# Full attention of a four-layer kernel: a new timetable of its tasks by beats, scores' two uses 24 beats apart, biases added by TensorE

## The chip, the cores and the metric

The kernel runs on one core of a Trainium2 chip. The metric is device time in microseconds (us) of one execution; a kernel is run several times and the median is compared.

## The reference

The input x has 16 batches of 512 tokens with 128 features. Four residual layers follow one another, each of the form x = x + layernorm(layer(layernorm(x))): windowed attention with 16 heads, a feed-forward layer with eight experts, full attention with 16 heads of 8 features, and a feed-forward layer with a sine. Only the third is changed:

```python
qkv = x @ Wqkv + bqkv                      # x: layernorm of the residual
q, k, v = split into 16 heads of 8         # rope on q and k
attn = softmax(q @ k.T * 8 ** -0.5)        # 512 x 512 for each head and batch, no mask
out = (attn @ v) joined to 128 features
return out @ Wout + bout
```

## The kernel before

The four layers run one after another. The third, `full_attention` (L873), works through the 16 batches with an order written out by hand: a loop over **beats** (L1161), 32 to a batch. Engines aren't locked to beats. A beat only says in which order instructions go into each engine's own queue, and every queue then runs in that order, as soon as what it waits for is there. SP (SyncE) has such a queue too, for nearly all transfers of this layer. I call the 32 beats in which batch b is attended the frame of b, and count beats 0 to 31 in it; z is the half of the heads (z=0 or 1).

In each beat three things run on the main road:

- `attend` (L1094): two matmuls (L1104) make scores transposed, with keys on partitions, and ScalarE (ACT) takes their exponential (L1110). Beats 0 to 15 use z=0, beats 16 to 31 use z=1.
- `score` (L1061) of a later batch: two matmuls (L1070) make the same scores with queries on partitions, and VectorE (DVE) takes each row's greatest (L1073). So scores are used twice: here for the maximum, and 32 beats later in `attend`, which gets the maximum as two extra rows of the contraction. I call these 32 beats the lead.
- `products` (L1113), every second beat: eight matmuls (L1118) multiply exponentials with values; a column of ones in the values gives the sums. It runs three beats behind.

Beside these, tasks are started at certain beats. They are generators; `yield n` puts what follows n beats later, and `run_due` (L202) goes through the tasks that are due at the end of each beat.

- `arrive(b+3)` (L966), from beat 10: GpSimd (POOL) gathers the experts' rows (`hb`, four indirect transfers, L972), makes `y` (four operations, L978), adds them (L983), normalizes (`normed_in`, L175: statistics by DVE, power and scaling by POOL) and adds to x (L986).
- `project(b+2)` (L988), from beat 0: normalizes x by POOL, transposes it (`tp_f`, L995, beat 6), multiplies with the weights (`pqk`, L1002, beat 8; bias by ACT in `qk`, L1008), makes values (`pv`, L1013, beat 10; bias by DVE into `vs`, L1017), and turns q and k by rope: three POOL operations for each of two halves (L1029 to L1032, beats 10 and 13). Each half is then cut into a high part (DVE, L964) and a rest (POOL, `cut`, L1035) and written to memory (`away`, L1038). From there 16 transfers of 128 KB load it in the layout that the scores need: four `qs` and four `ks` for z=0 (beat 20) and as many for z=1 (beat 23), all at L1056. Five pairs of buffers `qs`, `ks` go round. Zeroing them (L936, L937) is done while the experts run.
- `greatest(b+1, z)` (L1075), after the last score of a half (beats 15 and 31): a transpose (`pm`, L1081), a cut into `hi_m` and `lo_m` by DVE, and four small transfers that write these rows into `qs` (L1090).
- `put_away` (L1123), beats 2, 10, 18, 26: ACT copies products (`ou`, L1127), SP writes them (`heap`, L1128).
- `output(b-1)` (L1130), from beat 2: reads back sums and products (`sc`, `oc`, L1135, L1137, beat 4), DVE takes reciprocals (`rc`, L1140, beat 8), which go out and come back spread (`far`, `rb`, L1143, L1144), POOL multiplies (`oT`, L1147, beat 14), TensorE (PE) multiplies with the output weights (`pf`, L1151, beat 16), DVE adds the bias (`o`, tile `fo`, L1153), then `normed_in` and the residual sum (L1156).

One more thing orders the work. In the built program SP's transfers of this layer share eight completion semaphores in turn: with few exceptions a transfer isn't issued before the eighth transfer ahead of it has landed, and everything behind it in SP's queue waits too. `score` and `pm` take turns in two tiles of PSUM, so `score` of one beat waits for the `nm` reduction two tiles earlier.

Of the kernel before, what the change touches and what calls it, by code (L numbers as in the profile page):

```python
# [31 lines left out]
P = 128  # L32
# [142 lines left out]
def normed_in(net, x4, name, out, scale=None, mul=1.0, add=LN_EPS):  # L175
# [11 lines left out]
    nc.vector.tensor_scalar(v, mv[:, :, 1], mul, add, op0=ALU.mult, op1=ALU.add)  # L187
    r = net.small.tile([P, k], F32, name=f"r_{name}", tag="cr")
# [684 lines left out]
def full_attention(net):  # L873
# [20 lines left out]
    with ExitStack() as ctx:  # L894
# [15 lines left out]
        for half in range(2):  # L910
# [8 lines left out]
        vbias = wp.tile([P, 1, H1 * D1], F32, name="vbias")  # L919
        nc.sync.dma_start(  # L920
            out=vbias[:, 0, :], in_=a["L1_attn_bqkv"].rearrange("(o n) -> o n", o=1)[:, 2 * C :].to_broadcast([P, C])
        )
        wo = wp.tile([P, C], F32, name="wo1")
        nc.sync.dma_start(out=wo, in_=a["L1_attn_Wout"])
        bout = wp.tile([P, 1, C], F32, name="bout")
        nc.sync.dma_start(
            out=bout[:, 0, :], in_=a["L1_attn_bout"].rearrange("(o c) -> o c", o=1).to_broadcast([P, C])
        )
        ones_row = net.ones[: H1, :]

        qs = [wp.tile([P, HQ, T], F32R, name=f"qs{i}") for i in range(5)]
        ks = [wp.tile([P, HQ, T], F32R, name=f"ks{i}") for i in range(5)]
        for i in range(5):
            for r in range(2):

                nc.gpsimd.memset(qs[i][64 * r + 32 : 64 * r + 64, :, :].bitcast(F32), 0.0)  # L936
                nc.gpsimd.memset(ks[i][64 * r + 32 : 64 * r + 64, :, :].bitcast(F32), 0.0)  # L937
                for k in range(2):
                    nc.sync.dma_start(
                        out=ks[i][64 * r + KR + k : 64 * r + KR + k + 1, :, :].bitcast(F32), in_=ones_row  # L940
                    )
# [24 lines left out]
        def arrive(b):  # L966
# [3 lines left out]
            for j in range(NTB):  # L970
# [4 lines left out]
                )  # L975
            y = tok.tile([P, NTB, C], F32, name=f"y_{b}", tag="z")
# [5 lines left out]
            yield 11  # L982
            nc.gpsimd.tensor_tensor(y, y, hb, ALU.add)  # L983
            yield 4
            yield from normed_in(net, y, f"eo{b}", y)
            nc.gpsimd.tensor_tensor(xb, xb, y, ALU.add)  # L986

        def project(b):  # L988

            z = tok.tile([P, NTB, C], F32, name=f"z_f{b}", tag="z")  # L990
            yield from normed_in(net, net.x[b], f"f{b}", z)
            yield 3
# [19 lines left out]
            for i in range(NTB):  # L1012
                nc.tensor.matmul(  # L1013
                    pv[:, i, :], lhsT=zT[:, i * P : (i + 1) * P], rhs=raw[:, 2].rearrange("c h d -> c (h d)"),
                    start=True, stop=True,
                )
            nc.vector.tensor_tensor(  # L1017
                vs[b % 3][:, :, : VW * H1].rearrange("p i (h d) -> p i h d", d=VW)[:, :, :, :D1],
                pv.rearrange("p i (h d) -> p i h d", d=D1),
                vbias.to_broadcast([P, NTB, C]).rearrange("p i (h d) -> p i h d", d=D1),  # L1020
                ALU.add,
            )
            away = dp.tile([2, 2, 2, 2, 2, HD * HQ, T], F32, name=f"away_{b}", tag="away")
            cuts = []
            for half in range(3):

                if half < 2:
                    t1 = rp.tile([P, T], F32, name=f"t1_{b}_{half}", tag=f"t1{half}")
                    nc.gpsimd.tensor_tensor(t1, side[half], rope[:, 0, :], ALU.mult)  # L1029
                    t2 = rp.tile([P, T], F32, name=f"t2_{b}_{half}", tag="t2")  # L1030
                    nc.gpsimd.tensor_tensor(t2, side[1 - half], rope[:, 1, :], ALU.mult)  # L1031
                    nc.gpsimd.tensor_tensor(t1, t1, t2, ALU.add if half else ALU.subtract)  # L1032
                if half:
                    cut, t = cuts[-1]
                    nc.gpsimd.tensor_tensor(cut[:, 1, :], t, cut[:, 0, :], ALU.subtract)  # L1035
                    yield 1
                    for i in range(2):
                        nc.sync.dma_start(  # L1038
                            out=away.rearrange("k r z p h n t -> (k r z) n p h t")[:, :, i, half - 1, :],
                            in_=cut[:, i, :],  # L1040
                        )
                if half < 2:
                    yield 3
                    cut = rp.tile([P, 2, T], F32, name=f"cut_{b}_{half}", tag=f"cut{half}")
                    halves(cut[:, 0, :], t1)
                    cuts.append((cut, t1))
            yield 2
            for z in range(2):
                for kind, to in enumerate((qs, ks)):
                    for r in range(2):  # L1050

                        of = away[kind, r, z].rearrange("p h (d s) t -> p (h d) (s t)", s=HQ)
                        for i in range(2):
# [3 lines left out]
                                out=to[(2 * b + z) % 5][at : at + 2 * D1, :, :].bitcast(F32), in_=part  # L1057
# [3 lines left out]
        def score(b, k):  # L1061

            z, s, i = k // (HQ * NTB), k // NTB % HQ, k % NTB
            q, kk = qs[(2 * b + z) % 5], ks[(2 * b + z) % 5]
# [10 lines left out]
        def greatest(b, z):  # L1075
# [11 lines left out]
            for r in range(2):  # L1087
                for j, part in enumerate((hi, lo)):
                    at, of = 64 * r + KR + j, r * HQ * NTB
                    nc.sync.dma_start(  # L1090
                        out=qs[(2 * b + z) % 5][at : at + 1, :, :].bitcast(F32), in_=part[of : of + HQ * NTB, :]
                    )

        def attend(b, k):  # L1094
# [4 lines left out]
            q, kk = qs[(2 * b + s // HQ) % 5], ks[(2 * b + s // HQ) % 5]  # L1099
# [30 lines left out]
        def output(b):  # L1130
# [14 lines left out]
            yield 6  # L1145
# [4 lines left out]
            for j in range(NTB):  # L1150
                nc.tensor.matmul(pf[:, j, :], lhsT=oT[:, j * P : (j + 1) * P], rhs=wo, start=True, stop=True)  # L1151
            o = tok.tile([P, NTB, C], F32, name=f"fo_{b}", tag="fo")
            nc.vector.tensor_tensor(o, pf, bout.to_broadcast([P, NTB, C]), ALU.add)  # L1153
            yield 1
            yield from normed_in(net, o, f"fo{b}", o)
# [3 lines left out]
        BEATS = 2 * NG * NTB  # L1159
        with tc.manual_schedule():  # L1160
            for beat in range(-3 * BEATS, (B + 1) * BEATS):  # L1161
                b, k = divmod(beat, BEATS)

# [7 lines left out]
                if 0 <= b + 1 < B:  # L1171
                    score(b + 1, k)
                    if k % (BEATS // 2) == BEATS // 2 - 1:
                        tasks.append([beat, greatest(b + 1, 2 * k // BEATS)])
                if 0 <= pb < B and pk % 2 == 0:
                    products(pb, pk // 2)
                if k == BEATS - 22 and b + 3 < B:
                    tasks.append([beat, arrive(b + 3)])
# [161 lines left out]
```

## Time and profile before

| what | us |
|---|---|
| median of 3 runs | 2868.42 (2852.17 to 2899.47) |
| profiled execution: own time, span | 2889.88, 2888.1 |
| windowed attention, about 0 to 1110 | 1110 |
| experts, about 1110 to 1500 | 390 |
| full attention until its first attended beat, 1500 to 1634 | 134 |
| full attention, attended beats, 1634 to 2674 | 1040 |
| end of the last output, sine layer, 2674 to 2888 | 214 |

In the 1040 us of the attended beats the engines were busy: PE 889.90, DVE 693.29, ACT 593.83, POOL 401.94 us; the mean granted clock of PE was 0.81 of full speed. Busy shares are means over a batch, and PE's busy time includes stretches at half clock, so they do not show what a batch waits for. For that I read the waits of each engine, the chain of waits (what released what, followed back from the end), and the timeline of one batch. Beat 16 of batch 0 starts at 1673.5 us, beat 16 of batch 14 at 2583.8 us: 910.3 us for 14 batches. From batch 1 to batch 13 the distance is 65.2 us on average (62.0 to 68.4).

### The profile page before, as it was taken

How to read it: one execution, taken by the hardware profiler on the slowest of the kernel's cores; microseconds unless marked ns; L12 is line 12 of the kernel's file. 1: busy time of each engine (PE TensorE's matmuls, PEld its weight loads, DVE VectorE, ACT ScalarE, POOL GpSimd, SP SyncE). 2: the span in 40 equal slices, each digit the busy share in tenths (PEclk: the TensorE clock that was granted, in tenths of full speed). 3: DMA queues.
4: the chain of work that ended last, by engine and by line, in shares of the span. 5: the costliest groups of instructions: out<-in, count | busy, mean ns of one | idle time of the engine just before them, and what ended most of it. 6: DMA issues, size and time to landing. Idle time of an engine off the chain costs nothing. (4 is left out here: it accounts for less than half of the span.)

```text
span 2888.1 us, 54880 instructions
## 1 busy us (share of the span) xinstructions
PE 2252.4 (78%) x21335; PEld 1271.2 (44%) x21335; DVE 1865.8 (65%) x3711; ACT 1391.5 (48%) x3176; POOL 1410.3 (49%) x1399
## 2 busy tenths in 40 slices
PE   5888888989888882377771698888888888888676
PEld 2555555555555551366670233333333333332354
DVE  3676777777777754865411767667677767671576
ACT  1545554555455540232330156555555556566685
POOL 2555566565655546433324335444444444410598
PEclk7999999999999995576895568888888888896788
DMA  6555555555555531011112223223323323220001
GB/s 176 165 167 146 162 166 161 155 169 150 163 151 168 163 102 46 18 39 41 47 42 48 55 68 82 76 75 84 80 76 81 84 78 80 74 69 29 22 22 34
DMA packets 164288, 275.45 MB, mean 95 GB/s; under 512 B 20418, under 2 KB 64956, under 8 KB 158908
## 3 DMA queue, kind: packets, MB, share of 16 engines
q1 hardware_dynamic: 157696, 259.41, 31.5%
q0 software_dynamic: 4096, 8.40, 1.0%
q10 hardware_dynamic: 2236, 4.12, 0.5%
q8 instruction: 169, 2.77, 0.4%
q14 instruction: 91, 0.75, 0.1%
HBM read 133.55 MB, written 114.03 MB: 86 GB/s over the span
## 5 line engine op out<-in xcount | busy, mean ns | idle before, releaser
L1073 DVE TENSOR_REDUCE nm<-s 128x2 f32<-128x1024 f32 x512 | 613.4, 1221 | 207.5 <-PE s L1070 159.4
L1110 ACT ACTIVATE ex<-sT 128x512 f32<-128x512 f32 x1024 | 538.3, 601 | 400.9 <-PE sT L1104 388.1
L380 POOL TENSOR_TENSOR t<-t,t 128x512 f32<-128x512 f32 x256 | 319.6, 1269 | 381.4 <-DVE t L377 324.3
L431 ACT ACTIVATE pr<-s,nmax 128x96 f32<-128x96 f32 x1024 | 251.6, 356 | 324.5 <-DVE nmax L425 321.2
L1104 PE MATMUL sT<-qs,ks 50*128 50x512 f32 x1024 | 371.8, 548 | 37.1 <-ACT ex L1110 36.5
L1070 PE MATMUL s<-ks,qs 48*128 48x512 f32 x1024 | 315.3, 502 | 91.2 <-DMA ks<-away 63.8
L1118 PE MATMUL po<-ex,vs 128*32 128x512 f32 x2048 | 336.4, 736 | 0.0
L1104 PEld LDWEIGHTS sT<-qs,ks 50*128 50x128 f32 x1024 | 150.7, 212 | 386.0 <-ACT ex L1110 250.0
L371 PE MATMUL pq<-xnT,wqk 128*128 128x512 f32 x512 | 271.8, 656 | 23.3 <-DVE t L377 21.6
L375 DVE TENSOR_TENSOR t<-pq,rope 128x1024 f32<-128x1024 f32 x128 | 156.5, 1223 | 165.3 <-DMA far<-t 101.2
L443 POOL TENSOR_TENSOR pr<-pr,rc 128x768 f32<-128x768 f32 x128 | 188.0, 1468 | 55.1 <-DVE rc L442 49.8
L1070 PEld LDWEIGHTS s<-ks,qs 48*128 48x128 f32 x1024 | 137.6, 221 | 132.7 <-issue 74.0
L456 ACT COPY prT<-pt 96x512 f32<-96x512 f32 x256 | 138.8, 603 | 115.2 <-PE pt L454 115.2
L392 PE MATMUL pv<-wv,xnT 128*128 128x512 f32 x256 | 152.6, 681 | 29.0 <-ACT v_odd L396 29.0
L377 DVE TENSOR_TENSOR t<-pq,rope 128x1024 f32<-128x1024 f32 x128 | 155.5, 1215 | 0.0
L425 DVE TENSOR_REDUCE nmax<-s 128x8 f32<-128x768 f32 x128 | 118.2, 924 | 53.6 <-PE s L420 53.5
L454 PE MATMUL pt<-ident,pr 64*96 64x64 f32 x2048 | 85.7, 225 | 78.3 <-POOL pr L443 78.2
L485 PE MATMUL pf<-wo,oT 128*128 128x128 f32 x1024 | 131.1, 282 | 15.1 <-ACT v_odd L396 15.1
L371 PEld LDWEIGHTS pq<-xnT,wqk 128*128 128x128 f32 x512 | 92.9, 202 | 113.6 <-issue 97.0
L485 PEld LDWEIGHTS pf<-wo,oT 128*128 128x128 f32 x1024 | 124.2, 195 | 33.3 <-ACT v_odd L396 17.3
L725 PE MATMUL ph<-xT,w 128*128 128x128 f32 x512 | 97.6, 351 | 50.5 <-ACT hT L752 32.9
L471 PEld LDWEIGHTS po<-prT,v_even 96*64 96x64 f32 x2048 | 103.5, 137 | 75.7 <-issue 38.1
(258 smaller groups left out, 4158.2 us busy)
## 6 DMA issues: line engine op xcount, KB each, us to landing
far<-t SPq DMA_DIRECT2D x256, 256.0 KB
kT<-far SPq DMA_DIRECT2D x64, 512.0 KB
qT<-far SPq DMA_DIRECT2D x64, 512.0 KB
away<-cut SPq DMA_DIRECT2D x64, 256.0 KB
qs<-away SPq DMA_DIRECT2D x128, 128.0 KB
ks<-away SPq DMA_DIRECT2D x128, 128.0 KB
heap<-ou SPq DMA_DIRECT2D x64, 256.0 KB
v_even<-v_odd SPq DMA_DIRECT2D x32, 384.0 KB
```

What stands on the lines that cost most here:

```text
L371: nc.tensor.matmul(ps[:, s], lhsT=wqk[:, kind, 2 * half + g, s, :], rhs=xnT[b][:, :T], start=True, stop=True)
L375: nc.vector.tensor_tensor(t1, ps, rope[:, 0:1, :].to_broadcast([P, 2, T]), ALU.mult)
L377: nc.vector.tensor_tensor(t2, ps, rope[:, 1:2, :].to_broadcast([P, 2, T]), ALU.mult)
L380: nc.gpsimd.tensor_tensor(t1[:, s], t1[:, s], t2[:, 1 - s], ALU.add if s else ALU.subtract)
L431: nc.scalar.activation(pr[:, r, j, :], s[:, r, j * KW : (j + 1) * KW], AF.Exp, bias=nmax[:, r, j : j + 1])
L443: nc.gpsimd.tensor_tensor(pr, pr, per_token(rc, KW), ALU.mult)
L485: nc.tensor.matmul(pf[:, i, :], lhsT=o[:, p, j * P : (j + 1) * P], rhs=wo[:, NP * half + p, :], start=(p == 0), stop=(p == NP - 1),)
L1070: nc.tensor.matmul(ps[:, r, :], lhsT=q[rows, s, i * P : (i + 1) * P], rhs=kk[rows, s, :], start=True, stop=True)
L1073: nc.vector.tensor_reduce(nms[b, z][:, :, s, i], ps, AX.X, ALU.max, negate=True)
L1104: nc.tensor.matmul(t, lhsT=kk[rows, s % HQ, i * P : (i + 1) * P], rhs=q[rows, s % HQ, :], start=True, stop=True)
L1110: nc.scalar.activation(e, st[r], AF.Exp, scale=SCALE1)
L1118: nc.tensor.matmul(outs[-1][PADH * j : PADH * (j + 1), :], lhsT=vs[b % 3][:, i, VW * (NJ * g + j) : VW * (NJ * g + j) + PADH], rhs=weights ...
```

## The change

- The lead of `score` falls from 32 to 24 beats, and the pairs `qs`, `ks` from five to four.
- `project(b+2)` starts at beat 8 and its steps lie at other distances: `tp_f` at 16, `pqk` at 18, `pv` and the first half of rope at 20, the second at 23, cuts at 25 to 28, `away` at 27 and 29, loads for z=0 at 31, for z=1 at beat 2 of the next frame.
- `arrive` runs for batch b+4 from beat 28, one `hb` per beat; `y` at 0, sum at 5, normalization at 7 to 11, x at 12.
- `greatest` follows the earlier scores: its rows are issued at beats 26 (z=0) and 10 (z=1).
- `output` keeps its beats up to `rc` (8); `oT` is at 15, `pf` at 17, normalization at 20 to 24, x at 26.
- In this layer `normed_in` puts the power one beat behind the statistics (`apart=1`).
- The biases of values and output are added by one more matmul with a row of ones for each of four blocks; ACT copies the result out where DVE added before. The bias tiles hold one row instead of 128.

In SP's queue of the built program the order per batch becomes: `heap` (beat 2), eight z=1 loads, `sc`, `oc`, `far`, `rb`, `heap` (10), four rows of z=1, `heap` (18), `heap` (26), four rows of z=0, four `away`, eight z=0 loads. Before it was: eight z=0 loads, eight z=1 loads, two `heap`, four rows of z=1, `sc`, `oc`, `far`, `rb`, `heap`, two `away`, `heap`, two `away`, four rows of z=0.

```diff
-def normed_in(net, x4, name, out, scale=None, mul=1.0, add=LN_EPS):
+def normed_in(net, x4, name, out, scale=None, mul=1.0, add=LN_EPS, apart=0):
...
     nc.vector.tensor_scalar(v, mv[:, :, 1], mul, add, op0=ALU.mult, op1=ALU.add)
+    if apart:
+        yield apart
...
-        for i in range(5):
+        for i in range(NH):
...
         def arrive(b):
...
+                yield 1
             y = tok.tile([P, NTB, C], F32, name=f"y_{b}", tag="z")
...
-            yield 11
+            yield 5
             nc.gpsimd.tensor_tensor(y, y, hb, ALU.add)
-            yield 4
-            yield from normed_in(net, y, f"eo{b}", y)
+            yield 2
+            yield from normed_in(net, y, f"eo{b}", y, apart=1)
+            yield 1
             nc.gpsimd.tensor_tensor(xb, xb, y, ALU.add)
...
         def project(b):
...
-            yield from normed_in(net, net.x[b], f"f{b}", z)
-            yield 3
+            yield from normed_in(net, net.x[b], f"f{b}", z, apart=1)
+            yield 4
...
-                    start=True, stop=True,
+                    start=True, stop=False,
                 )
-            nc.vector.tensor_tensor(
+                nc.tensor.matmul(pv[:, i, :], lhsT=net.ones[:1, :], rhs=vbias, start=False, stop=True)
+            nc.scalar.copy(
...
+            for half in range(2):
...
+                ts.append(t1)
+                yield 3 - half
+            for half in range(2):
+                cut = rp.tile([P, 2, T], F32, name=f"cut_{b}_{half}", tag=f"cut{half}")
+                halves(cut[:, 0, :], ts[half])
+                yield 1
+                nc.gpsimd.tensor_tensor(cut[:, 1, :], ts[half], cut[:, 0, :], ALU.subtract)
+                yield 1
+                for i in range(2):
+                    nc.sync.dma_start(
...
-            yield 6
+            yield 7
             oT = op.tile([P, T], F32, name=f"oT1_{b}", tag="oT")
...
+                nc.tensor.matmul(pf[:, j, :], lhsT=net.ones[:1, :], rhs=bout, start=False, stop=True)
...
-            nc.vector.tensor_tensor(o, pf, bout.to_broadcast([P, NTB, C]), ALU.add)
-            yield 1
-            yield from normed_in(net, o, f"fo{b}", o)
+            nc.scalar.copy(o, pf)
+            yield 3
+            yield from normed_in(net, o, f"fo{b}", o, apart=1)
+            yield 2
...
+        LEAD = 24
...
-            for beat in range(-3 * BEATS, (B + 1) * BEATS):
+            for beat in range(-4 * BEATS, (B + 1) * BEATS):
                 b, k = divmod(beat, BEATS)
+                sb, sk = divmod(beat + LEAD, BEATS)
...
-                if k == BEATS - 22 and b + 3 < B:
-                    tasks.append([beat, arrive(b + 3)])
-                if k == 0 and 0 <= b + 2 < B:
+                if k == 28 and b + 4 < B:
+                    tasks.append([beat, arrive(b + 4)])
+                if k == 8 and 0 <= b + 2 < B:
                     tasks.append([beat, project(b + 2)])
```

## The prediction

> **What bounds the kernel now.** Engines' busy shares first: in the attended beats PE is busiest, with 889.9 of 1040 us, but at a mean clock of 0.81, so I looked for what makes it wait. The waits of PE between 1640 and 2600 us (total, times, longest) name two:
>
> ```profile
> PE pf L1151 <- POOL oT L1147: 71.6, 12, 6.0
> PE s L1070 <- DMA ks<-away: 25.9, 16, 5.5
> ```
>
> Once in a batch PE stands 6.0 us because `oT` comes late from POOL, and once because the loads of `ks` have not landed. The chain of waits over one batch (start, us, what) shows that both lie on one ring:
>
> ```profile
> 1988.10 1.93 PE pqk L1002 x4
> ...
> 1990.88 1.27 POOL t L1029
> ...
> 1999.76 1.73 POOL y L978 x4
> ...
> 2006.50 1.23 POOL oT L1147
> 2007.77 2.08 PE pf L1151 x8
> ...
> 2022.90 12.91 DMA ks<-away
> ```
>
> From `pqk` POOL works without a gap through rope, the four `hb`, `y`, rope again, a cut, and only then `oT`; then come the second cut, `away`, the loads, and the next batch's scores. So a batch lasts as long as this ring, 65.2 us, not as long as PE's work. SP's timeline of the same batch shows what the loads do to the transfers behind them:
>
> ```profile
> 2019.21 3.65 SPq L1056 DMA_DIRECT2D qs<-away  x4
> 2022.90 1.80 SPq L1056 DMA_DIRECT2D ks<-away  x4
> 2025.45 10.66 SPq L1056 DMA_DIRECT2D qs<-away  x4
> 2036.17 1.78 SPq L1056 DMA_DIRECT2D ks<-away  x4
> 2042.79 2.48 SPq L1128 DMA_DIRECT2D heap<-ou  x2
> 2047.40 0.57 SPq L1090 DMA_DIRECT2D qs<-hi_m  x1
> 2049.88 0.54 SPq L1090 DMA_DIRECT2D qs<-lo_m  x1
> ...
> 2052.42 0.57 SPq L1135 DMA_DIRECT2D sc<-heap  x1
> ```
>
> Call the first load's issue t0 = 2019.2. The z=0 loads have landed at t0+17 (the score that waits for `ks` starts at 2036.34). The four z=1 `qs` loads land one after another: the issues that wait for their semaphores stand at t0+23.6, +26, +28.2 and +30.7 (2042.79, its second some 2.1 us later, 2047.40, 2049.88), and the `ks` loads with the last, about +31. SP's own waits say the same of the whole layer:
>
> ```profile
> SPq L1056 <- DMA qs<-away: 123.8, 57, 4.1
> ...
> SPq L1128 <- DMA qs<-away: 88.0, 28, 4.4
> SPq L1090 <- DMA qs<-away: 63.0, 32, 4.3
> ```
>
> The reader should see that for some 31 us after t0 SP's queue is shut for anything eight transfers behind. Today that hurts nobody, since t0 comes early: `sc` is issued at t0+33 and `rc`, `oT` come later still.
>
> Last, the clock. PE's timeline before and after the second wait (start, us, what):
>
> ```profile
> 2032.08 1.06 PE L1118 MATMUL po<-ex,vs 128*32 128x512 f32 x8
> 2033.08 0.49 PE L1104 MATMUL sT<-qs,ks 50*128 50x512 f32 x2
> 2036.34 1.28 PE L1070 MATMUL s<-ks,qs 48*128 48x512 f32 x2 [2.77 <-DMA ks<-away]
> ...
> 2047.71 1.94 PE L1118 MATMUL po<-ex,vs 128*32 128x512 f32 x8
> ```
>
> Eight `po` take 1.06 us before the wait and 1.94 us still 11 us after it: half clock. Two beats take 2.85 us at full clock (`po` at 2017.76 to `po` at 2020.61) and 4.49 us at half (2043.22 to 2047.71). 32 beats at full clock would be 46 us.
>
> **The change part by part.**
>
> *POOL's order.* `hb` and `y` (4 x 0.98 + 1.73 us), and the first rope, cut and second rope no longer stand ahead of `oT`. This takes away the wait of 6.0 us as it is now. About one POOL operation per beat: POOL has 402 us of work in 1040 and stays far from a bound.
>
> *Biases.* 8 more matmuls each in `pv` and `pf`, 128 columns wide but one row deep. No row of the trace is one row deep; the nearest is `pf` itself, 2.08 us for eight at half clock, so about 1.1 at full. Bounds: nothing, if short rows pipelined away, and 2 x 2.1 us at half clock. I take 1.1 us each. DVE loses 0.69 + 0.68 us, ACT gains two copies of 0.59. Both have cover: DVE is busy 693 and ACT 594 of 1040 us. Fewer memsets (4 x 1.80 us of POOL at 1109 to 1145 us) and narrower bias tiles cost and gain nothing, since the experts' search on DVE sets the pace there.
>
> *From beat 16 to t0.* Now `tp_f`, `pf`, `pqk`, `pv` all lie in the second half of the frame. I count at full clock from the start of beat 16: beat and scores 0.9, `tp_f` 1.0 (0.97 in the chain at 1984.31), beat 17 with products 1.95, `pf` with biases 2.2, beat 18 0.9, `pqk` 1.93: 8.9. `qk` by ACT 2 x 0.68: 10.3. POOL: first rope 3.8, 14.1. Next in POOL's queue is the power `r_fo`, whose statistics DVE makes at beat 21, behind `pv` and the reductions, at about 16; 1.04, so 17; second rope 3.8, `fo` 1.75, x 1.28, two cuts 2.54: 26.5. `away` takes 5.0 to 5.2 in the chain, less what its first part overlaps: t0 at +31. The beats themselves arrive at 32 after 16 x 1.43 + 1.0 + 2.2 + 1.9 + 2.2 = 30. So t0 falls at beat 32, eight beats before the first score that needs it (beat 40); today it is ten beats, and there already it isn't enough.
>
> *From t0 to the next beat 16.* Three consumers wait. (1) `score` of beat 40: eight beats are 11.5 us, the loads need 17; PE stands 5 to 6 us, at full clock. (2) `sc`: in SP's queue it now stands right behind the z=1 loads, so it is issued at t0+23, and lands 2.04 us later (the last batch's row): t0+25.2. `rc` (0.54 us) stands in DVE's queue at beat 8 (40), reached at 17 + 0.5 + 1.2 + 1.1 (statistics) = t0+20. DVE stands 5 us there. Behind it are the reductions of beats 9 and on; with two PSUM tiles PE gets one score further and stands too. (3) `far` needs the third `qs` load, `rb` the fourth (+30.7) and takes 3.0: `oT` at +35. The z=1 rows of the maximum come behind `rb` on the semaphores of the `ks` loads: issued by +33.5, there by +35.5, for beat 16. Lead 24 leaves them 6 beats, where 32 left 14. Meanwhile DVE after `rc` needs 7 reductions (8.5) and 2.5 to 3 us of statistics and cuts: 25.8 + 11 = +36 to +37. All agree: beat 16 starts at t0+36.
>
> *The ring and the clock.* 31 + 36 = 67 us, against 65.2 now. It is a full-clock sum. Two waits of about 5 us per batch drop the clock. The Trainium skill's page "TensorE: Matmul & The Clock Gate", Part 1 (the HAM clock gate), says that an idle window of about 3.4 us halves the clock and a busy window of about 3.4 us restores it. By that rule each wait costs 3.4 x (1 - 2.85/4.49) = 1.2 us, half of it hidden in beats that wait anyway, 1.2 us in all. The row differs: after the wait shown, which at 2.77 us is shorter than a window, the clock stayed at half for over 11 us. If each wait brought 20 us of it, 14 us would be lost, half hidden: 7. I take 2.5, nearer the rule, because after the 6.0 us waits of today `po` is back at 1.0 us within 7 us (2014.74). That gives 69.5 us per batch (68.2 by the rule, 74 by the longest row).
>
> *The ends.* Batch 0 needs 8 beats of scores less before its first attended beat (8 x 1.23 by the `nm` row = 10), its first wait for loads (5.5 us) overlaps with them, and `arrive(1)` now stands ahead of `project(0)` on POOL (hb, y, power: some 6 us on the way to the first load, half of it hidden): 13 us earlier. The tail I leave as it is; the first batch has no `output`, 4 us.
>
> **Sum**, against the profiled execution: 14 batches were 910.3 us; now 14 x 69.5 - 4 = 969; with -13 at the start, +46 us: 2889.9 becomes 2936. That execution lies 21.5 us above the median of the runs, so for the median I say 2868.4 + 46 = 2914 us.
>
> **The rivals.**
>
> *A, the forecast*: ring of 66.5 to 71.5 us, so +4 to +74: 2870 to 2940. For it: SP's waits. Chance 0.45.
>
> *B, the change does what it says*: the loads are early enough, no wait of SP reaches DVE or PE. Then 32 beats (46) with `tp_f`, `pqk`, `pv`, `pf`, `pm` (8) are 54 us: 14 x 54 - 910 - 17 = -171: 2697. If only (2) and (3) fail to appear and (1) stays, 61 us: -73, 2795. Against it: t0+17 is measured in this trace with less in the way. It decides if t0 comes 5 beats earlier than I find. Chance 0.13 for faster by over 2%.
>
> *C, the clock stays low*: 74 us, +109: 2977; 76 us with the POOL chain late by another beat or two: 3005. For it: half clock for 11 us after 2.77 us of idling. Chance 0.30.
>
> *D, no difference*: t0 two or three beats earlier, ring 65 to 66: 2850 to 2870. Against it only that POOL's `r_fo` waits for beat 21. Chance 0.12.
>
> **How the numbers follow.** Runs of this kernel differ by 1.6%, so less than about 2% can't be told from no change. Slower by over 2% is above 2926: C and the upper quarter of A: 0.43. Faster is B: 0.13. The rest, 0.44. The range leaves out most of B and the end of C: 2820 to 3000. A alone: 2870 to 2940.
>
> **What would show it.** The wait of `pf` for `oT` gone or under 2 us; `rc` waiting for `sc<-heap` about 5 us in most batches; the first z=0 score waiting 5 us or more for `ks<-away` at beat 8; `sc` issued 23 us after t0; z=1 rows the last release of beat 16; 15 to 28 us at half clock per batch. I am wrong if t0 lies at beat 28 or earlier, if `sc` comes before the z=1 loads have landed, or if DVE does not wait at `rc`.

## The result, and the profile after

After the change the median of four runs is **3211.05 us** (3203.48 to 3214.76) against 2867.36 us (2852.17 to 2899.47) of the kernel before: a ratio of 1.1215, 95% interval 1.1165 to 1.1265. The forecast was 2914, and its range ended at 3000. The profiled execution of the kernel after took 3210.98 us (span 3209.2).

From beat 16 of batch 0 (1664.4 us) to beat 16 of batch 14 (2874.8) it takes 1210.4 us, where before took 910.3: 300 of the 321 us between the spans lie there. The waits of the kernel after, 1640 to 3000 us (total, times, longest):

```profile
DVE rc L1137 <- DMA sc<-heap: 198.1, 15, 31.7
...
PE s L1067 <- DVE nm L1070: 177.9, 17, 13.8
...
PE s L1067 <- DMA ks<-away: 95.2, 14, 8.5
...
PE pf L1148 <- POOL oT L1144: 11.8, 1, 11.8
```

The wait of `pf` for `oT` (71.6 us before) is gone but for one. In its place PE stands twice a batch: some 7 us until `ks` has landed, then 13 us for the reduction, because DVE stands some 13 us at `rc` until `sc` is there. SP's timeline of one batch (start, us, what), to be read beside the one of before:

```profile
2389.59 3.48 SPq L1053 DMA_DIRECT2D qs<-away  x4
2393.12 1.79 SPq L1053 DMA_DIRECT2D ks<-away  x4
2395.39 0.34 SPq L1125 DMA_DIRECT2D heap<-ou  x1
2399.77 6.18 SPq L1053 DMA_DIRECT2D qs<-away  x4
2406.00 1.78 SPq L1053 DMA_DIRECT2D ks<-away  x4
2411.91 0.57 SPq L1132 DMA_DIRECT2D sc<-heap  x1
2414.45 0.56 SPq L1134 DMA_DIRECT2D oc<-heap  x1
2421.93 0.34 SPq L1140 DMA_DIRECT2D far<-rc  x1
```

t0 is 2389.6, and `sc` is issued at t0+22.3, as forecast. But it doesn't land 2 us later. The chain of waits has the next links, and then what TensorE does until the next batch (start, us, what):

```profile
2411.91 9.35 DMA sc<-heap
...
2421.35 0.55 DVE rc L1137
...
2425.48 1.87 PE po L1115 x8
...
2441.54 0.73 PE pf L1148 x2
2442.27 0.72 PE pf L1149 x2
...
2448.48 3.71 PE pqk L1004 x4
...
2459.11 0.99 PE po L1115 x8
...
2472.46 6.82 DMA away<-cut
```

`sc` takes 9.35 us from issue to landing. PE has stood 12.9 us when it starts again at 2423.8, and then eight `po` take 1.87 us, twice their 0.99: half clock. It stays so until `pqk` has run, at 2453.6. The one-row biases (L1149) take as long as `pf` itself (L1148).

The same as a table, means of one frame over the frames 2 to 13, worked out from the records of each run: length, time at half clock, and idle time of PE in gaps of over 0.5 us.

| label | what it is | median us | ratio to before (95%) | frame | half | idle |
|---|---|---|---|---|---|---|
| before | | 2850 to 2872 | 1 | 64.5 | 20.5 | 7.0 |
| after | | 3211.05 | 1.1215 (1.1165 to 1.1265) | 86.8 | 47.5 | 20.3 |
| e1 | after, z=1 loads later | 3012.66 | - | 72.9 | 35.0 | 6.5 |
| e2 | after, loads spread | 3007.48 | 1.0473 (1.0397 to 1.0549) | 71.9 | 27.9 | 9.0 |
| e3 | after, lead 32 | 3158.60 | 1.1036 (1.0974 to 1.1099) | 79.4 | 63.7 | 0.7 |
| e4 | after, biases on DVE | 3032.96 | 1.0594 (1.0546 to 1.0641) | 77.1 | 31.6 | 21.3 |
| e5 | before, biases on PE | 2962.17 | 1.0324 (1.0246 to 1.0403) | 71.2 | 37.1 | 2.4 |
| e6 | after, biases 128 rows high | 3067.23 | 1.0752 (1.0681 to 1.0823) | 80.8 | 38.4 | 20.9 |
| e7 | e3, biases 128 rows high | 2910.21 | 1.0151 (1.0048 to 1.0253) | 66.1 | 17.9 | 8.2 |
| e8 | e3, biases on DVE | 2862.01 | 1.0036 (1.0012 to 1.0059) | 62.8 | 14.2 | 8.1 |
| e9 | e8, `qs` loads spread | 2761.55 | 0.9681 (0.9630 to 0.9732) | 58.6 | 15.1 | 2.6 |
| e10 | before, `qs` loads spread | 2759.33 | 0.9697 (0.9638 to 0.9756) | 58.2 | 7.1 | 5.5 |
| e11 | e4, z=1 loads later | 2864.41 | 1.0054 (1.0025 to 1.0083) | 65.8 | 22.8 | 8.9 |
| e12 | after, `rc` later | 3061.64 | 1.0775 (1.0704 to 1.0845) | 77.9 | 41.6 | 7.6 |
| e13 | e3, biases 32 rows high | 3139.21 | 1.0964 (1.0896 to 1.1032) | 80.3 | 68.0 | 0.0 |
| e14 | e3, biases 96 rows high | 2920.46 | 1.0196 (1.0134 to 1.0258) | 65.7 | 17.1 | 8.1 |
| e15 | before, layout | 2781.34 | 0.9702 (0.9651 to 0.9752) | 58.3 | 7.1 | 5.5 |
| e16 | e8, layout | 2722.95 | 0.9516 (0.9464 to 0.9567) | 54.6 | 6.8 | 1.7 |
| e17 | e3, work added behind `pf` | 3082.74 | - | 76.9 | 37.0 | 6.6 |
| e18 | e4, layout | 2829.56 | 0.9905 (0.9878 to 0.9933) | 64.0 | 17.9 | 9.1 |

Runs of one kernel can lie over 1.5% apart, so ratios are of the faster ones alone, and where too few of these were left (e1 with 2964 to 3028 us, e17 with 3037 to 3088) the medians are to be compared with those of before beside them, 2865.55 and 2855.45. The frame of before is that of the execution of 2889.88 us.

### The profile page after: what moved, and what is told of

It reads as the page before. It is cut to its first block, busy times and chain, and to the rows that moved or that the text cites. A ratio compares the mean times of both kernels' runs of the same rounds, so it can differ in the third digit from the quotient of the medians.

```text
span 3209.2 us, 55398 instructions
## 1 busy us (share of the span) xinstructions
PE 2428.7 (76%) x21591; PEld 1353.7 (42%) x21591; DVE 1866.8 (58%) x3679; ACT 1409.8 (44%) x3208; POOL 1410.6 (44%) x1395
## 4 chain that ended last, share of the span: by engine, by line
PE 22%; DMA 17%; DVE 6%; POOL 4%; ACT 2%; issue 1%; SPq 0%; POOLq 0%; DVEq 0%; ACTq 0%
DMA qs<-away 9%; PE po L1115 7%; PE sT L1101 6%; DMA sc<-heap 4%; DVE nm L1070 3%; DMA away<-cut 3%; PE s L1067 3%; PE pqk L1004 2%; PE pf L1148 1%; PE pf L1149 1%; ACT ex L1107 1%; PE pv L1019 1%; PE pv L1015 1%; POOL go L199 1%; DMA ks<-away 1%
## 5 line engine op out<-in xcount | busy, mean ns | idle before, releaser
L1067 PE MATMUL s<-ks,qs 48*128 48x512 f32 x1024 | 347.6, 537 | 312.6 <-DVE nm L1070 187.4
L1101 PE MATMUL sT<-qs,ks 50*128 50x512 f32 x1024 | 400.6, 595 | 33.1 <-ACT ex L1107 31.3
L1115 PE MATMUL po<-ex,vs 128*32 128x512 f32 x2048 | 367.1, 798 | 0.0
L1101 PEld LDWEIGHTS sT<-qs,ks 50*128 50x128 f32 x1024 | 164.2, 233 | 403.3 <-ACT ex L1107 223.3
L1067 PEld LDWEIGHTS s<-ks,qs 48*128 48x128 f32 x1024 | 155.5, 245 | 347.1 <-DVE nm L1070 204.8
L373 PE MATMUL pq<-xnT,wqk 128*128 128x512 f32 x512 | 271.4, 655 | 21.3 <-DVE t L379 19.1
L394 PE MATMUL pv<-wv,xnT 128*128 128x512 f32 x256 | 156.3, 696 | 27.9 <-ACT v_odd L398 27.9
L1028 POOL TENSOR_TENSOR t<-qk,rope 128x512 f32<-128x512 f32 x32 | 40.8, 1276 | 254.6 <-ACT qk L1010 254.6
L487 PE MATMUL pf<-wo,oT 128*128 128x128 f32 x1024 | 132.4, 284 | 15.1 <-ACT v_odd L398 15.1
```

The source lines that it names most:

```text
L373: nc.tensor.matmul(ps[:, s], lhsT=wqk[:, kind, 2 * half + g, s, :], rhs=xnT[b][:, :T], start=True, stop=True)
L394: nc.tensor.matmul(pv, lhsT=xnT[b][:, WIN + j * P : WIN + (j + 1) * P], rhs=wv[:, half * T : (half + 1) * T], start=True, stop=True,)
L487: nc.tensor.matmul(pf[:, i, :], lhsT=o[:, p, j * P : (j + 1) * P], rhs=wo[:, NP * half + p, :], start=(p == 0), stop=(p == NP - 1),)
L1067: nc.tensor.matmul(ps[:, r, :], lhsT=q[rows, s, i * P : (i + 1) * P], rhs=kk[rows, s, :], start=True, stop=True)
L1101: nc.tensor.matmul(t, lhsT=kk[rows, s % HQ, i * P : (i + 1) * P], rhs=q[rows, s % HQ, :], start=True, stop=True)
L1115: nc.tensor.matmul(outs[-1][PADH * j : PADH * (j + 1), :], lhsT=vs[b % 3][:, i, VW * (NJ * g + j) : VW * (NJ * g + j) + PADH], rhs=weights ...
```

## The experiments

**First four: the change's parts, one at a time.** Theory T came from the chain above: the z=1 loads stand ahead of `sc` in SP's queue and on the transfers' way, DVE stands in order at `rc`, PE idles, and the clock drops. R1: the biases do it. R2: a lead of 24 is too short by itself.

e1, the z=1 loads later:

```diff
-                yield 3
+                yield 3 if z else 12
```

> The kernel after, with one number changed: the eight loads of the second half (z=1) are issued nine beats later, so that sc, oc, far, rb and the rows of z=0 stand ahead of them in SP's queue. Timetable, lead of 24 beats and TensorE biases stay. Theory T (sc is issued behind the z=1 loads, and its packets wait behind theirs; VectorE stands at rc, TensorE idles over 10 us and runs at half clock for some 25 us after it): sc lands about 2 us after its issue, VectorE's wait at rc falls from 31.7 us to under 5, the idle time of TensorE at the negated maximum (13.8 us a batch) goes, the wait of the first score for ks (8.5 us) stays; a batch takes 66 to 72 us in place of 88, the whole 2850 to 2980. Theory R1 (the one-row bias matmuls cost or hold down the clock): hardly a change, 3150 or more. Theory R2 (scores only 24 beats ahead are enough by themselves, by the rows due six beats after the last score): the idle time moves from the negated maximum to the rows of beat 16, 3100 or more.

e2, another order of rows for `qs` and `ks`, which spreads each `qs` load over more DMA engines (`part` and `of` follow it):

```diff
-                        of = away[kind, r, z].rearrange("p h (d s) t -> p (h d) (s t)", s=HQ)
+                        of = away[kind, r, z].rearrange("p h (d s) t -> (h d) p (s t)", s=HQ)
```

> The kernel after, with the rows of each qs load written in another order of its dimensions, so that its packets are spread over eight DMA engines where the trace of after shows two; number, size and place of the loads stay. Theory T: a qs load takes 0.7 to 1.3 us in place of 2.5, all loads have landed 12 to 15 us after the first was issued in place of 31, sc lands 2 to 3 us after its issue, both idle times of TensorE (8.5 us at ks, 13.8 us at the negated maximum) shrink to under 2 us each; a batch takes 55 to 62 us, the whole 2700 to 2840. R1 (biases): 3100 or more, since the biases are untouched. R2 (lead alone): the rows of beat 16 are last instead, 2950 to 3100.

e3, the lead alone undone:

```diff
-        NH = 4
+        NH = 5
-        LEAD = 24
+        LEAD = 32
-                if k == 28 and b + 4 < B:
+                if k == 20 and b + 4 < B:
-                if k == 8 and 0 <= b + 2 < B:
+                if k == 0 and 0 <= b + 2 < B:
```

> The kernel after, with the lead alone undone: scores 32 beats ahead, five buffers, project and arrive eight beats earlier; the order of GpSimd's work and the TensorE biases stay. T: the z=1 loads have been issued some nine beats ahead of sc, so sc lands in about 2 us and VectorE waits at rc under 5 us; ks is there before the first score; pf waits no longer for oT. A batch takes 57 to 64 us, the whole 2720 to 2860. R1 (biases): 3100 or more. R2 gives the same as T here.

e4, the biases alone undone (for `pf`, and in the same way for `pv`):

```diff
-                nc.tensor.matmul(pf[:, j, :], lhsT=net.ones[:1, :], rhs=bout, start=False, stop=True)
-            nc.scalar.copy(o, pf)
+            nc.vector.tensor_tensor(o, pf, bout.to_broadcast([P, NTB, C]), ALU.add)
```

> The kernel after, with the biases alone undone: they are added by VectorE again, as before; timetable and lead of 24 stay. T: both idle times stay (8 and 13 us a batch); TensorE is freed of eight one-row matmuls a batch, 0.36 us each at half clock, 3 us a batch: 3120 to 3190. R1 (the biases cause it): the half-clock time falls from 51 us a batch to about 20 and the whole to under 2950.

All four missed T's numbers. In e1 the wait at `rc` is gone (0.7 us in all up to 2600 us), and so are the 13 us of PE: idle time falls from 20.3 to 6.5 us a frame. That part of T holds, and is worth 198 us by the medians (228 by e1's two faster runs). But the frame is 72.9 us, not 66 to 72, since half clock still takes 35.0. e2 moved less than its expectation, because each `ks` load, which had landed 0.3 us after the one before it, now came 1.0 us after it; the loads landed at t0+20, not t0+12 to 15, and `sc` still stood behind them. Its time lies in the range that R2 gave, but not for R2's reason: no wait of PE in e2 ends with the rows of the maximum.

e3 and e4 speak against T alone. e3 has no idle time left and is slow all the same; T expected under 2860 us, R1 3100 or more, and it took 3158.6. e4 keeps all the idle time (21.3 us a frame) and gains 178 us, 11 a batch, where T gave the matmuls' own time 3 us a batch. So R1 has a part in it that isn't this time. Engines' busy time and granted clock in three stretches of e3 (from, to, length, PE busy (instructions), PEld, DVE, ACT, POOL, PEclk, ...):

```profile
2104.30:2107.20 2.90, 2.67 (x21) 0.95 (x17) 2.46 (x3) 2.06 (x4) 0.00 (x0) 1.00 0.00 0
...
2112.30:2166.90 54.60, 54.60 (x196) 18.52 (x196) 35.50 (x58) 26.81 (x51) 19.09 (x27) 0.50 0.34 88
2170.60:2173.30 2.70, 2.70 (x18) 0.95 (x17) 1.23 (x1) 2.47 (x5) 1.70 (x2) 1.00 0.00 0
```

By its records PE is busy for 54.6 us without a gap, and all of it at half clock. The Trainium skill's page "TensorE: Matmul & The Clock Gate", Part 1 (the HAM clock gate), says that a stretch of about 3.4 us of busy PE restores the clock. Here sixteen such stretches didn't. The timeline of PE shows what stood at either end (start, us, what):

```profile
2106.19 1.07 PE L1115 MATMUL po<-ex,vs 128*32 128x512 f32 x8
2107.19 0.49 PE L1148 MATMUL pf<-wo,oT 128*128 128x128 f32 x2
2107.61 0.48 PE L1149 MATMUL pf<-bout,ones 1*128 1x128 f32 x2
...
2113.45 1.93 PE L1115 MATMUL po<-ex,vs 128*32 128x512 f32 x8
...
2164.24 1.93 PE L1115 MATMUL po<-ex,vs 128*32 128x512 f32 x8
...
2167.25 3.48 PE L1004 MATMUL pqk<-zT,wqk 128*128 128x512 f32 x4
...
2171.32 1.06 PE L1115 MATMUL po<-ex,vs 128*32 128x512 f32 x8
```

The clock drops behind `pf` with its one-row biases and comes back with `pqk`, whose matmuls fill 128 rows and 128 columns. The records carry the active rows and columns of each matmul, so I worked out **occupancy**: rows times columns times the time in which the columns stream, as a share of 128 x 128 over 3.41 us (the step in which the records' clock changes). Streaming time at full clock is 0.21 us for 512 columns of `s` and `sT`, 0.43 for the others (two passes), after the spacing of their records, and twice that at half clock. In the first six traces two thresholds fit: at half clock a stretch above 0.74 is followed by full clock, at full clock one below 0.35 by half. Steady beats have about 0.67 at half clock (two beats hold 4 `sT`, 4 `s` and 8 `po`, which are 800 + 768 + 2048 columns of the full array with `po` in two passes; in 4.49 us some 5400 could stream): too little to lift it. At full clock the same beats have about 0.52, enough to keep it. I call this theory C (it is not the rival C of the prediction).

**Is it the one-row biases?** e5 puts them, alone, into the kernel before (e4's diff the other way round).

> The kernel before with one part of the change alone: the biases added by one-row matmuls of TensorE; timetable, lead of 32 beats and buffers of before stay. Theory C, formed from the four runs so far: the granted clock goes by how much of the 128x128 array the matmuls of a 3.41 us stretch occupy (active rows times active columns, as the records name them), not by busy time. In the records a stretch at half clock is followed by full clock when it holds more than about 0.74 of the array, one at full clock by half when it holds less than about 0.35; the steady beats hold about 0.67 at half clock, so they cannot lift it themselves, and a one-row matmul holds next to nothing, so it takes away the lift that pf gives and pushes the clock down behind pv. C: half clock from pf to the next pqk, 60 us a batch or more where before has 20, with all of the waits of before in place: 3100 to 3260. Theory T alone (queue waits; the one-row matmuls cost only their own time, under 6 us a batch): 2870 to 2960.

e6 and e7 make them 128 rows high, with as many matmuls; e6 on after, e7 on e3 (the values of the other 127 rows are zero):

```diff
-        bout = wp.tile([1, C], F32, name="bout")
-        nc.sync.dma_start(out=bout, in_=a["L1_attn_bout"].rearrange("(o c) -> o c", o=1))
+        bout = wp.tile([P, C], F32, name="bout")
+        nc.vector.memset(bout, 0.0)
+        nc.sync.dma_start(out=bout[:1, :], in_=a["L1_attn_bout"].rearrange("(o c) -> o c", o=1))
...
-                nc.tensor.matmul(pf[:, j, :], lhsT=net.ones[:1, :], rhs=bout, start=False, stop=True)
+                nc.tensor.matmul(pf[:, j, :], lhsT=net.ones, rhs=bout, start=False, stop=True)
```

> The kernel after with the bias matmuls widened from one row to 128: ones of 128 rows against a bias tile whose other 127 rows are zero, so as many matmuls, of the same length, with all rows active. Waits, lead and timetable stay. C: pf and pv with their biases now fill the array, so the clock comes back behind pf as it does in before; the half-clock time falls from 51 us a batch to some 20 to 27, the idle times (8 and 13 us) stay; 3010 to 3100, near the version with the biases on VectorE (3033). If the rows do not matter (the one-row matmuls cost by their number): within 1% of after, 3180 to 3240.

> The kernel after with the lead undone (32 beats, five buffers) and the bias matmuls widened to 128 rows. Against the 3158.6 of the same kernel with one-row biases this changes nothing but the number of active rows. C: half clock falls from some 66 us a batch to under 25, there is no idle time left above 3 us, a batch takes 57 to 63 us: 2700 to 2840. If the rows do not matter: 3130 to 3190.

e8 is e3 with the biases on DVE, so of the change only the timetable of the tasks is left: the order of POOL's work, and with it the beats of SP's transfers.

> The kernel after with lead and biases undone: of the change only the order of GpSimd's work is left, with scores 32 beats ahead and the biases on VectorE. C and T together: pf waits no longer for oT (6.0 us a batch in before), the loads stand well ahead of sc, nothing pulls the clock down but the start of a frame; a batch takes 56 to 62 us in place of 65.2: 2690 to 2820. If the new order of GpSimd's work is itself a cost (a rival of the prediction): above 2880.

Rows matter: e6 gains 144 us on after, e7 248 us on e3, by rows that are zero. In e7 half clock falls from 63.7 to 17.9 us a frame. Its timeline around `pf`, to be read beside e3's:

```profile
2132.73 1.06 PE L1117 MATMUL po<-ex,vs 128*32 128x512 f32 x8
2133.72 0.49 PE L1150 MATMUL pf<-wo,oT 128*128 128x128 f32 x2
2134.05 0.39 PE L1151 MATMUL pf<-bout,ones 128*128 128x128 f32 x2
...
2138.15 1.06 PE L1117 MATMUL po<-ex,vs 128*32 128x512 f32 x8
```

And the stretch behind it, with the columns as in e3:

```profile
2137.10:2148.00 10.90, 10.19 (x62) 3.52 (x63) 10.62 (x19) 8.05 (x17) 6.32 (x6) 1.00 0.42 133
```

Two things differ. The clock stays at 1.00. And the matmuls of `pf` follow each other faster: the next pair starts 0.33 us and then 0.22 us later, where in e3 it is 0.42 each time. C's sizes were off, though. e5 lost some 100 us (3.2%), not 250 to 400: half clock rose only to 37.1 us a frame, since in nine of the frames 1 to 13 the beats behind `pf` ran at full clock all the same. e7 and e8 stayed 70 and 42 us above their expected ranges, for another reason: PE now waits for `ks` in every frame. The line of e8 (1640 to 2600 us):

```profile
PE s L1072 <- DMA ks<-away: 99.1, 14, 7.5
```

So the new timetable takes away `pf`'s wait for `oT` (6.0 us) and brings one for `ks` (7.1 us, before 1.6): nothing gained, 1.0036.

**Rows or form, and is it the clock?** e13 and e14 take 32 and 96 rows (`net.ones[:32, :]`, `bout[:32, :]`, and so on).

> The kernel after with the lead undone and the bias matmuls 32 rows high (1 row: 3158.6, 128 rows: 2910.2). If the form with fewer rows than its neighbour is slow by itself: pairs start 0.213 us apart at full clock as with one row. Then the share of the array that a stretch of pf with biases holds at full clock is 0.107 us of streaming by 0.213 us, times 160 of 256 rows, 0.31: under 0.35, so the clock drops behind pf and pv as with one row: 3060 to 3170. If pairs start 0.112 us apart, the share is 0.60 and the clock holds: 2890 to 2960.

> The same with bias matmuls 96 rows high. At 0.213 us from start to start the share is 0.107 by 0.213, times 224 of 256 rows, 0.44: over 0.35, so the clock holds behind pv and pf at full clock, and what is lost against 128 rows is the longer pairs alone (32 matmuls by 0.1 us, 3 us a batch): 2910 to 3000. At 0.112 us apart: 2890 to 2940. If only the full 128 rows keep the clock: above 3060.

32 rows cost what one row costs, 96 rows what 128 do, and the pairs' spacing goes the same way: the median distance of two matmuls of `pf` at full clock is 0.213 us with 1 and 32 rows, 0.113 with 96 and 0.112 with 128. So spacing and rows didn't come apart here. e17 asks about the clock by itself: it leaves the one-row biases, rows and spacing, as they are and adds work.

```diff
+            for i in range(2):
+                nc.tensor.matmul(both[:, 1], lhsT=wo, rhs=oT, start=True, stop=True)
```

> The kernel after with the lead undone and one-row biases (3158.6), and added work: behind pf of each batch two more matmuls of 128 rows, 128 columns and 512 elements into an unused bank, whose result nobody reads. At half clock they take 3.7 us (as the four records of pqk do, which have the same shape), a whole stretch of 3.41 us at full occupancy. If the clock goes by occupancy: it comes back behind pf as it does behind pqk, half-clock time falls from 66 us a batch to 25 to 40, and the kernel gets faster by work that is added: 2930 to 3060. If the loss is the one-row matmuls' own length and spacing: 16 times 2 to 4 us more, 3190 to 3220.

It got faster by work that is added: 3158.6 to 3082.7 by the medians, 76 us and not 100 to 230, and 122 us by its fastest run (3036.98). The timeline of a run of 3082.83:

```profile
1989.16 1.94 PE L1115 MATMUL po<-ex,vs 128*32 128x512 f32 x8
...
1996.09 0.79 PE L1150 MATMUL pf<-bout,ones 1*128 1x128 f32 x2
1996.82 3.78 PE L1152 MATMUL pf<-oT,wo 128*128 128x512 f32 x4
2002.97 1.06 PE L1115 MATMUL po<-ex,vs 128*32 128x512 f32 x8
```

`po` takes 1.94 us ahead of the added matmuls and 1.06 behind them. Half clock falls to 37.0 us a frame; the rest of the gain is taken by the wait for `ks`, which comes back (6.6 us of idle time), as in e7. With the thresholds left as fitted on the first six traces, the next clock is foreseen for 5048 of the 5125 stretches of the 14 later ones, where "it stays" would be right for 4459, and for 630 of the 666 changes. A second count, over the attended beats alone, puts the streaming near the end of each matmul's record. It gives 4257 of 4344 stretches and 422 of 504 changes, with thresholds of 0.75 and 0.37 from the first six. Other measures, each with its own best thresholds, foresee fewer of these 504: rows alone 356, streaming time alone 278, columns alone 196. So the product of rows, columns and time fits best of what was tried; what the clock really goes by is inferred from this fit. Of the 248 us between e3 and e7 the closer spacing is 52 to 82 us (32 matmuls a batch, 0.10 us each at full clock or 0.16 at half, 16 batches); the rest goes with the clock (45.8 us of half clock a frame less). For after itself, where e6 gave back 144 us, the two weren't tried apart.

**The queue.** e12 leaves loads and `sc` where they are, and moves `rc` behind nine more beats:

```diff
-            yield 4
+            yield 13
...
-            yield 7
+            yield 5
```

> The kernel after, with rc, far and rb nine beats later and pf seven beats later; loads, sc, lead and biases stay where they are, so sc still lands some 9 us after its issue. If the second idle time is VectorE standing in order at rc with the negated maxima behind it, this wait and the 13.8 us of TensorE at the negated maximum go, the first wait for ks (8 us) stays: 2980 to 3080. If the loads themselves hold up the scores (contention at the memory or PSUM): the idle time stays and the whole is above 3150.

As T has it: 3061.6 us, idle time 7.6 us a frame, with the loads and `sc` as they were. DVE's order is what carries the delay of `sc` to PE. Where the 9.35 us come from the transfers' packets show: of `sc`'s 128 packets of 256 bytes 112 start within 1.9 us of the issue, the other 16 not before 8.2 us, in each of ten batches. In e1, where no loads are ahead, all start within 2.4 us. The semaphore of `sc` says the same: in one batch 14 of its 16 increments come 1.8 to 2.1 us after the issue, the last two at 9.1 and 9.3 us. A `qs` load is 16 packets of 8 KB at 0.31 us each, and takes 2.5 us, so two DMA engines carry it, and its semaphore gets two increments when it lands (eight in e2); 16 of 128 are two of 16 engines' share, and behind the three loads of 2.5 us that are still on their way that is where `sc` waits. The Trainium skill's page "DMA: Bandwidth & Descriptors", section "Why a DMA increments its semaphore by 16 and not by 1", says that a transfer takes the largest number of engines, up to 16, that divides the outermost dimension of both sides. Its section "Rules for kernel authors" says that a leading broadcast of c copies leaves at most c engines. These packets agree, with c = 2.

e11 asks if queue and biases are two causes: e4 and e1 in one.

> The kernel after with two things altered at once: the z=1 loads nine beats later, and the biases on VectorE again. Each alone took 198 us and 178 us off. If the two causes are separate, the savings add: 2810 to 2870. If they are two names for the same half-clock time (each of them alone gives back the same loss): 2950 to 3010.

They nearly add: 2864.4 within 2810 to 2870, where the savings of e1 and e4 together would give 2835 (2805 with e1's two faster runs). e9 and e10 then spread the `qs` loads alone, on e8 and on before. There the rows of `qs` stand in another order than those of `ks`, so the scores are those of other pairs of rows; loads, shapes and order are the same.

> The version with lead and biases undone (2862.0), with the qs loads, and these alone, written in the order of dimensions that spreads their packets over eight DMA engines; the ks loads stay as they were. There the only idle time left is the first score's wait for ks, 7.0 us a batch, because ks lands 17 us after the first load is issued, behind four qs loads of 2.5 us each; behind it the clock drops for 7 to 14 us. Spread, the qs loads take about 1 us each, so ks lands 9 to 10 us after the first load: the wait should go, and most of the drop with it. A batch takes 54 to 57 us in place of 61.8: 2740 to 2800. Were the loads not what binds (rival: the order of GpSimd's work puts the score late by itself): 2840 or more.

> The kernel before with the qs loads alone spread over eight DMA engines. The first score of a frame waits 1.5 us for ks there, and pf 6.0 us for oT behind the rotary work on GpSimd. The 1.5 us and part of the half clock of the frame's first 14 us should go, the 6.0 us stay: 2790 to 2850. If oT's wait is what the loads set (rb lands late behind them): 2740 to 2790.

They took 100 and 91 us off. e15 (on before) and e16 (on e8) reach it with the rows in order, by another layout of `away`:

```diff
-            away = dp.tile([2, 2, 2, 2, 2, HD * HQ, T], F32, name=f"away_{b}", tag="away")
+            away = dp.tile([2, 2, 2, HD, 2, 2, HQ, T], F32, name=f"away_{b}", tag="away")
...
-                            part = of[i : i + 1].to_broadcast([2, D1, HQ * T]) if kind == 0 else of
+                            part = of[:, i : i + 1].to_broadcast([D1, 2, HQ * T]) if kind == 0 else of
```

> The kernel before, with away kept in another order of its dimensions, so that each qs load spreads over eight DMA engines while each ks load stays one piece of 16 rows; the same bytes, loads and timetable, no other change. From the earlier run with spread loads (2759.3): 2745 to 2785. If the write to away, which now takes another pattern, is slower than before, oT and ks come late again: 2790 to 2860.

> The version with lead and biases undone (of the change only GpSimd's order), with the same layout of away. From the earlier run with spread loads (2761.6): 2745 to 2790, so no better than the kernel before with the layout. If GpSimd's order gains once the loads are out of the way, 20 us or more below the run of the kernel before with this layout.

e15 takes 2781.3 us and e16 2723.0, faster than both kernels. With this layout the new timetable gains 58 us (e16 against e15). With spread loads alone it gained nothing: e9 and e10 are 2 us apart. Both e9 and e16 have their sixteen loads landed at t0+21 to t0+22, not t0+31 (medians, by the semaphores), but the layout also shortens the write to `away`. SP's timeline of one batch of e9, then of e16 (start, us, what):

```profile
2010.25 3.35 SPq L1046 DMA_DIRECT2D away<-cut  x4
2017.83 4.10 SPq L1059 DMA_DIRECT2D qs<-away  x4
```

```profile
2002.96 2.56 SPq L1046 DMA_DIRECT2D away<-cut  x4
2006.87 3.01 SPq L1058 DMA_DIRECT2D qs<-away  x4
```

From the last `away` to t0 it takes 5.4 us in e9 and 1.9 in e16 (medians of eleven batches). In e9 PE still waits for `ks` and `qs` where the frame starts, 25 us in all between 1640 and 2450 us, and half clock takes 15.1 us a frame against 6.8. On before the shorter write gains nothing (e15 and e10 have frames of 58.3 and 58.2 us). That it is what lets e16 gain fits these numbers, but it was not tried by itself. Last, e18 is e16 with the lead of 24.

> The kernel after with biases on VectorE and the layout that spreads the qs loads; lead of 24 and GpSimd's order stay. With 32 beats this version took 2723.0. If the lead of 24 costs nothing by itself: 2700 to 2750. If the loads, shorter but still ahead of sc and of the first score eight beats later, keep PE waiting 2 to 4 us a batch and drop the clock for one or two stretches: 2760 to 2850.

2829.6 us, 107 us more than e16. The line of its waits (1640 to 2600 us) says why:

```profile
DVE rc L1142 <- DMA sc<-heap: 94.0, 14, 7.7
```

`sc` still stands behind eight loads, and PE idles 9.1 us a frame. So R2 has this much in it: with 24 beats the z=1 loads fall just ahead of `sc`, and shorter loads don't change the order. With the old layout, once these loads are moved, 24 beats take what 32 take (e11 2864.4, e8 2862.0): there it is the order that matters. With the new layout this was not tried.

## Why the prediction was wrong

- **`pf`'s wait goes, `sc` is issued at t0+23, three consumers wait.** Right for all but the third consumer: one wait of `pf` in the whole layer, `sc` at t0+22.3, DVE at `rc` in 15 places, the first score's wait for `ks` 6.8 us (95.2 / 14; forecast 5 to 6). The rows of z=1, forecast as the last release of beat 16, end no wait of PE in after; only in e12, with `rc` out of the way, do they end 14 waits, 26.4 us in all.
- **"and lands 2.04 us later (the last batch's row): t0+25.2".** This step failed. The row was taken from a place with no loads on their way; with three `qs` loads in front, `sc` lands 9.35 us after its issue. I had seen that loads shut SP's queue, but not that, once issued, a transfer still stands behind their packets. So DVE stands 13 us at `rc` and not 5, and from t0 to beat 16 it takes 47 us (2389.6 to 2436.3), not 36.
- **"I take 1.1 us each" for the biases.** Failed, and so did the bound of 2.1. In the chain above `pf` with biases takes 5.8 us at half clock (2441.54 to 2447.33) where `pf` alone took 2.08. The nearest row was eight matmuls with like neighbours; one-row matmuls between 128-row ones nearly double the distance (0.374 us for 0.213 at half clock).
- **"I take 2.5" for the clock.** This step failed in its mechanism, not only in its size. Half clock takes 47.5 us a frame where 15 to 28 were forecast and before had 20.5. I weighed the clock only as something that a wait brings, and looked for how long a wait lasts. It is brought, and kept, by what the matmuls are: e4 has the same waits and 31.6 us, e3 no waits and 63.7. From beat 16 to the next t0 it took 41 us (2436.3 to 2477.7), not 31, the first 17 of them at half clock.
- **The sum.** 69.5 us a batch were forecast, 86.5 measured (1210.4 / 14). The biases cost 178 us in all (after against e4), 11.1 a batch, where 2.2 stood in the sum: 8.9. Of these some 5.8 are the clock, by an estimate: e4 has 15.9 us less of half clock a frame, and each loses 1 - 2.85 / 4.49. `sc` takes 7.3 us longer than it was given, and e1 agrees: its 198 us are 12.4 a batch, of which the forecast had 5. Together 16.2 of the missing 17.0, so near in part by chance, since a share of a whole run and the length of one transfer are added.
- **The rivals.** The prediction's C, the clock stays low, named the right resource, but its price (74 to 76 us) came from waits alone. B's 54 us a frame can be had (e16, 54.6), but e16 has neither this lead nor these biases, and a layout that B did not have.

What stays open: why pairs with 1 and 32 rows start twice as far apart as with 96 and 128, and why the one-row biases cost some 100 us in the timetable of before and 297 us in e3's (e3 against e8). Whether a stretch of 3.41 us holds `pf` alone or `pf` and `po` may differ between the two; that was not tried by itself.

## What to carry to other kernels

Take the duration of a moved transfer from a place with the same traffic in front of it, and ask which engine of another kind stands in order behind the instruction that waits for it. Before small matmuls are added to PE, ask how much of the array they fill: here the steady loop was just too thin to lift the clock, the few dense matmuls lifted it, and thinning them cost far more than their own time. What an edit gains by taking away one wait can't be told until the next one on the ring is known, as e8 shows.

## What the hardware did that was not expected

- PE, busy without a gap by its records, stayed at half clock for 54.6 us, and the clock returned behind four dense matmuls (e3: `po` 1.93 to 1.06 us; e17 in the same way). Occupancy of the array over 3.41 us with thresholds of about 0.74 and 0.35 foresees some 98% of the stretches, where "it stays" is right for 87%.
- A matmul of one row took as long as its neighbour of 128 rows (0.72 us for two of either, at half clock), and both stood nearly twice as far apart as matmuls of 128 rows do: 0.213 us at full clock with 1 or 32 rows, 0.112 with 96 or 128.
- Work added to PE made the kernel faster: 3158.6 to 3082.7 us (medians; 3037.0 in its fastest run).
- A transfer of 32 KB took 9.35 us instead of some 2, since an eighth of its packets started some 6.5 us after the others, with loads of 128 KB, carried by two engines each, in front of it.
